# The feed-forward product of two batches by seven block products, with the sums of its weight blocks kept in DRAM and streamed

## The chip, the cores and the metric

The kernel runs on one core of one Trainium2 chip. The core has a matrix engine (PE, with its weight loads shown apart as PEld), a vector engine (DVE), a scalar engine (ACT), a third engine for elementwise work (POOL), and a queue (SP) from which nearly all DMAs are issued. The metric is the device time of one execution in microseconds (us); three executions of the kernel before gave 829.0, 829.38 and 829.86 us, median 829.38.

## The reference

There are 16 batches of 128 rows and 1024 columns. Each is normalised and goes through a cross attention with 32 query heads of width 32 and 8 key/value heads, with a residual; then the sum is normalised again and goes through one matrix product, again with a residual:

```python
x = x + xattn(layernorm(x), ctx, ctx, Wq, bq, Wk, bk, Wv, bv, Wo, bo)
x = x + scale * (x_ei @ kernel)        # x_ei: layernorm(x), its last 20% of columns times -4
```

`kernel` is a 1024 x 1024 matrix of zeros and ones (one in ten is a one). All the rest is float32. The second product is called the FFN below.

## The kernel before, in words

**Tiling.** Two batches make a group; there are eight groups. Of each group the kernel computes keys and values (`prep_k`, `prep_v`), queries (`prep_q`), the attention of four units (one batch and one half of the heads each: `scores`, `exponentials`, `divide`, `turn`, `weighted`), the output projection (`out_proj`) and the FFN (`ffn_transpose`, `ffn`).

**Seven products.** The query and output projections of a group are products of two-by-two blocks: 512 rows or columns of the weight against the halves of the two batches. `seven` (L385) does them by seven block products in place of eight. Each product accumulates in a PSUM tile, and `read` on DVE adds it to one of the four result blocks. The tile `u` takes products 1, 3, 5 and 7, and is read between them, so that product 3 can only start when the read after product 1 is over, and likewise 5 after 3 and 7 after 5. Product 2 has a tile of its own; products 4 and 6 share a third (`v`), which takes the buffer of product 2's tile (`ps_mm` has two buffers), so that product 4 waits for the read of product 2, and product 6 for that of product 4. Three of the seven products use plain weight blocks and four use sums of blocks. The sums are computed once (`combine`, L665), written to DRAM (`sums`) and streamed.

**The stream of weights.** `want` lists 512 KB pieces in the order in which they will be used; `fetch` (L202) issues the next piece's DMA into a ring of eight (`RING`) each time a piece has been used.

**The FFN before** takes each batch by itself. `ffn_transpose` (L614) turns the normalised rows by PE, ACT copies each half to a rounded copy `x2h` (type float32r), and DVE subtracts it to leave the remainder `x2l`. `ffn` (L630) multiplies both by the whole weight, which stays in SBUF in float32r (`wf_sb`): per batch two column halves, eight chunks, two parts, so 32 matmuls of 128 x 128 by 512. DVE then scales each half and adds the residual (L638).

**The order of the work** is written out ahead of time by a planner, `Stream` (L23). It keeps a clock, `now`. Dense work (products) comes from generators that give the time of each piece; `later(us, fn)` sets an event. Before each piece the events that are due are issued in the order of their due times. So every engine has one fixed queue in program order. A unit of attention issues its 32 score matmuls, adds 1.2 to the clock, sets four `exponentials` at 0.7, 3.1, 5.5 and 7.9 us after that, each `divide` 2.3 us behind its own, and each `turn` 9.25 us behind it in most groups (`length / 2 - 3`); it runs dense work until `length - 2` (22.5) us have passed, and closes with `weighted`, which adds 1.0. Groups 1 to 5 have this order, in the driver's `elif more` branch (L804 to L817): `out_proj` of the group before with `prep_ctx`, `prep_k`, `prep_v` with the four FFN transposes in it, the FFN of the two batches before, then `prep_x` and the queries of the next group. The third unit of a group begins just after the last value matmuls:

```python
mixed(prep_v(nxt), chain(ffn_transpose(p0), ffn_transpose(p1)), 1, 2),
once(get_x, nxt * GB + 1, 5.0),
```

`mixed(dense, light, skip, every)` puts a piece of the second generator behind each `every`th piece of the first, from number `skip` on. Group 6 has no FFN of its second batch, group 7 has units of 12 us, and the rest of the FFN stands at the end.

**Buffers.** Loaded rows are in `xn` (3 buffers), residuals in `x` (3), the FFN's parts in `x2h` and `x2l` (2 each), attention outputs in `yT` (7). The 0/1 weight is loaded as bytes (`load_ffn`) and converted on ACT (`convert_ffn`).

## Time and profile before

| what | value |
|---|---|
| median of three executions | 829.38 us |
| profiled execution: its time, its span | 829.15 us, 827.4 us |
| PE busy | 806.2 us, 97% of the span |
| DVE, ACT, POOL busy | 441.4 (53%), 350.7 (42%), 69.5 (8%) us |
| DMA | 165.14 MB, 200 GB/s over the span, q1 59% of the 16 engines |
| one group in the steady part (groups 2 to 5) | 100.2 us |
| last group (group 7), and what follows it | 58.8 us, 52.6 us |

The span is the time from the first instruction to the last; the 1.75 us between it and the execution's own time lie around it. In lists of groups of instructions, the first numbers are busy time in us and mean ns of one, and behind the second bar stands the idle time of the engine ahead of them and what ended it. In a timeline the columns are start and duration in us, engine, line, operation, output and inputs. Durations of DVE, ACT and PE overlap a little with the next instruction, so that the spacing of starts, not the duration, says what a row of instructions costs. A float32 matmul shows as two records, a float32r matmul as one.

### The profile page before, as it was taken

What the parts mean: (1) busy time and instruction counts of PE and PEld (TensorE: products, weight loads), DVE (VectorE), ACT (ScalarE), POOL (GpSimd) and SP (SyncE); (2) the same over time, 40 slices, a digit from 0 to 9 for tenths busy, and PEclk for the clock granted to TensorE, in tenths of its full rate; (3) what the DMA queues carried; (4) which work ended last, traced back from release to release, by engine and by line L of the source; (5) the groups of instructions that cost most, each with busy time, mean ns of one, the idle gap of its engine ahead of it and who ended that gap; (6) DMA issues with size and microseconds to landing.
All of it is one profiled execution on the core that took longest, in us unless ns stands there. A gap on an engine that the chain in (4) does not pass through costs nothing.

```text
span 827.4 us, 14055 instructions
## 1 busy us (share of the span) xinstructions
PE 806.2 (97%) x5344; PEld 606.9 (73%) x5344; DVE 441.4 (53%) x830; ACT 350.7 (42%) x1313; POOL 69.5 (8%) x110
## 2 busy tenths in 40 slices
PE   5999999999999999999999999999999999999997
PEld 4887884779757796588965889558895679756556
DVE  0469656555455554546564454654456555467442
ACT  1245854544335443445333543344434454366200
POOL 1000020002000020000200002000110002000300
PEclk9999999999999999999999999999999999999999
DMA  8899887416874088631886238860488407762511
GB/s 295 278 363 367 281 307 245 161 52 227 275 237 152 27 280 259 225 128 62 278 275 214 90 116 266 279 218 38 158 268 261 154 26 256 238 220 76 190 65 76
DMA packets 74082, 165.14 MB, mean 200 GB/s; under 512 B 5120, under 2 KB 33792, under 8 KB 74016
## 3 DMA queue, kind: packets, MB, share of 16 engines
q1 hardware_dynamic: 73728, 163.60, 59.0%
q8 instruction: 42, 0.69, 0.3%
q0 software_dynamic: 288, 0.66, 0.3%
q14 instruction: 24, 0.20, 0.1%
HBM read 147.46 MB, written 16.78 MB: 199 GB/s over the span
## 4 chain that ended last, share of the span: by engine, by line
PE 92%; DVE 2%; ACT 2%; issue 2%; DMA 1%; POOL 0%; SPq 0%; ACTq 0%; DVEq 0%; POOLq 0%
PE o_u L585 13%; PE f L282 13%; PE q_u L374 12%; PE tpp L524 7%; PE o_v L585 7%; PE q_v L374 6%; PE k L282 6%; PE v L282 6%; PE sc L491 4%; PE av L534 4%; PE q L282 3%; PE o_c L585 3%; PE q_c L374 3%; PE tp_f L624 2%; PE tp_x L299 1%
## 5 line engine op out<-in xcount | busy, mean ns | idle before, releaser
L507 ACT ACTIVATE p<-sc,negm 128x128 f32<-128x128 f32 x512 | 180.9, 369 | 163.2 <-DVE inv L518 97.1
L526 ACT COPY pt<-tpp 128x512 f32<-128x512 f32 x128 | 74.8, 592 | 91.6 <-PE tpp L524 91.3
L507 ACT ACTIVATION_READ_ACCUMULATOR p<-sc,negm 128x1 f32 x512 | 105.8, 207 | 0.0
L282 PE MATMUL f<-wf_sb,x2l 128*128 128x512 f32 x256 | 105.4, 412 | 0.0
L503 DVE TENSOR_REDUCE negm<-sc 128x4 f32<-128x512 f32 x128 | 86.7, 682 | 33.8 <-PE sc L491 33.7
L282 PE MATMUL f<-wf_sb,x2h 128*128 128x512 f32 x256 | 101.1, 395 | 0.0
L519 DVE TENSOR_TENSOR p<-p,inv 128x512 f32<-128x512 f32 x128 | 89.8, 701 | 4.4
L524 PE MATMUL tpp<-ident,p 128*128 128x128 f32 x512 | 77.4, 274 | 6.3 <-ACT pt L526 3.4
L374 PE MATMUL q_u<-t,piece 128*128 128x128 f32 x672 | 81.2, 275 | 0.0
L524 PEld LDWEIGHTS tpp<-ident,p 128*128 128x128 f32 x512 | 60.6, 141 | 25.3 <-issue 12.3
L374 PEld LDWEIGHTS q_u<-t,piece 128*128 128x128 f32 x672 | 78.0, 192 | 0.1
L282 PE MATMUL v<-wv_sb,cT 128*128 128x256 f32 x256 | 65.3, 390 | 4.9 <-DMA wv_sb<-in_L_xattn_Wv_dram 4.6
L166 POOL TENSOR_TENSOR x<-x,bo_b 128x256 f32<-128x256 f32 x64 | 48.2, 784 | 156.3 <-DMA x<-in_x_dram 154.9
L585 PE MATMUL o_v<-piece,s 128*128 128x512 f32 x128 | 60.2, 597 | 0.0
L585 PE MATMUL o_u<-piece,s 128*128 128x512 f32 x128 | 59.0, 593 | 0.0
L585 PE MATMUL o_u<-piece,yT 128*128 128x512 f32 x128 | 58.5, 599 | 0.0
L282 PE MATMUL k<-cT,wk_sb 128*128 128x256 f32 x256 | 58.3, 380 | 0.0
L282 PEld LDWEIGHTS f<-wf_sb,x2l 128*128 128x128 f32 x256 | 48.1, 188 | 11.0 <-issue 1.1
L282 PEld LDWEIGHTS f<-wf_sb,x2h 128*128 128x128 f32 x256 | 48.2, 188 | 10.3 <-issue 0.5
L542 ACT COPY yT<-av 128x512 f32<-128x512 f32 x32 | 18.7, 585 | 86.0 <-PE av L534 86.0
L282 PEld LDWEIGHTS v<-wv_sb,cT 128*128 128x128 f32 x256 | 47.1, 196 | 10.8 <-issue 5.0
L282 PEld LDWEIGHTS k<-cT,wk_sb 128*128 128x128 f32 x256 | 47.8, 190 | 9.0 <-issue 2.6
(80 smaller groups left out, 979.6 us busy)
## 6 DMA issues: line engine op xcount, KB each, us to landing
piece<-o SPq DMA_DIRECT2D x64, 512.0 KB, 4.6
piece<-q SPq DMA_DIRECT2D x56, 512.0 KB, 4.3
piece<-in_L_xattn_Wq_dram SPq DMA_DIRECT2D x50, 512.0 KB, 4.8
piece<-in_L_xattn_Wo_dram SPq DMA_DIRECT2D x48, 512.0 KB, 4.6
xn<-in_x_dram SPq DMA_DIRECT2D x16, 512.0 KB, 5.7
x<-in_x_dram SPq DMA_DIRECT2D x16, 512.0 KB, 5.6
out_dram<-x SPq DMA_DIRECT2D x16, 512.0 KB, 2.8
ctx<-in_ctx_dram SPq DMA_DIRECT2D x15, 512.0 KB, 7.2
```

What stands on the lines that cost most here:

```text
L166: lambda cut=cut: nc.gpsimd.tensor_add(x_t[:, cut], x_t[:, cut], bo_b[:, cut]) and None,
L282: nc.tensor.matmul(mm, lhsT=lhsT, rhs=rhs, start=k == 0, stop=k == n - 1)
L374: nc.tensor.matmul(mm if part is None else mm[:, part], lhsT=lhsT, rhs=rhs, start=start and n == k == 0, stop=k == len(some) - 1, skip_gro ...
L491: nc.tensor.matmul(tiles[i][:, g], lhsT=qT[rows, g], rhs=kT[rows, a, cols], start=True, stop=True,)
L503: nc.vector.tensor_reduce(negm, tile_, AX.X, ALU.max, negate=True)
L507: nc.scalar.activation(p[:, g], tile_[:, g], AF.Exp, bias=negm[:, g : g + 1], accum_out=total[:, g : g + 1],)
L519: nc.vector.tensor_mul(p, p, inv.unsqueeze(2).to_broadcast([P, NG, S]))
L524: nc.tensor.transpose(tp[:, g], p[:, g], ident)
L526: nc.scalar.copy(pt, tp)
L534: nc.tensor.matmul(mm[i * HD : (i + 1) * HD], lhsT=vs[b][:, h * HD : (h + 1) * HD], rhs=pts[i], start=True, stop=True,)
L542: nc.scalar.copy(yTs[b, a], mm)
L585: nc.tensor.matmul(mm, lhsT=lhsT[:, 2 * k + c], rhs=w[:, c], start=start and k == c == 0, stop=k == c == 1, skip_group_check=True,)
```

## The change

The FFN of a group is now done for both batches together by `seven`. Its left blocks are the halves of the two batches' normalised rows, its right blocks are the quarters of the weight. Three quarters (`b11`, `b21`, `b22`) stay in SBUF as float32r; the four sums are computed once on DVE from the byte weights, written to DRAM, and streamed through the ring like the other weights: eight pieces more for each group.

The transposes are now copied to `x2T` in float32 (ACT). Seven left operands (`a11`, `a12`, `a22` and four sums, made by DVE) are each split into a rounded copy by ACT and a remainder by DVE. `prepare` sets eight such steps as events; three more splits are set when products 1, 2 and 3 are done. `prepare` is issued in `prep_v`, behind the transposes, three pieces before its end.

Moved or resized around that: rows and residuals share one tag, `rows`, with seven buffers; both row loads of the next group are issued when a group begins and normalised 9 and 19 us later (before: 14 us, and 5 us after `prep_v`); two of the FFN transposes go into `prep_k`; the sums of Wq and Wo are handled and written as halves of 256 KB; `convert_ffn` starts after the last sums of Wo; the FFN of group 5 as a whole goes to group 7, those of groups 6 and 7 to the end; the first context tile and Wv are loaded by one DMA each instead of two; `bo_b` is loaded from SP, behind the first rows, instead of from POOL; `yT` has six buffers.

```diff
-    XB = 3
+    ROWS = 7
...
-    wf_sb = const.tile([P, NC, F], FR, name="wf_sb")
+    wf = {n: const.tile([P, NC // 2, HALF], FR, name=f"wf_{n}") for n in ("b11", "b21", "b22")}
...
-    load_ctx(0, 2)
-    for half in (slice(0, NC // 2), slice(NC // 2, NC)):
-        nc.sync.dma_start(
-            out=wv_sb[:, half], in_=Wv.rearrange("(c p) n -> p c n", p=P)[:, half]
-        )
+    load_ctx(0)
+    nc.sync.dma_start(out=wv_sb, in_=Wv.rearrange("(c p) n -> p c n", p=P))
...
-    nc.gpsimd.dma_start(out=bo_b, in_=bo.partition_broadcast(P))
     nc.gpsimd.dma_start(out=fscale, in_=ffn_scale.partition_broadcast(P))
+    nc.sync.dma_start(out=bo_b, in_=bo.partition_broadcast(P))
...
+        def convert(dst, c, cols):
+            src = raws[c // HC][:, c % HC, cols]
+            nc.scalar.activation(dst[:, c % HC], src, AF.Copy, scale=weights[c])
+
+        for c in range(HC):
+            stream.later(4.0 * c, lambda c=c: convert(wf["b11"], c, low))
+            stream.later(4.0 * c + 1.3, lambda c=c: convert(wf["b21"], c + HC, low))
+            stream.later(4.0 * c + 2.6, lambda c=c: convert(wf["b22"], c + HC, high))
+
+        def sums_of(k):
...
+            for (n, c), src in t.items():
+                cols = slice(c % 2 * HALF, (c % 2 + 1) * HALF)
+                nc.sync.dma_start(out=sums["f", n, k][:, cols], in_=src.bitcast(FP))
+
+        spread(sums_of(0), 1.8, lambda: spread(sums_of(1), 1.8))
...
-            cut = slice(4 * h, 4 * h + 4)
-            nc.scalar.copy(hi[:, cut], tp)
-            nc.vector.tensor_tensor(lo[:, cut], tp, hi[:, cut], ALU.subtract)
+            x2Ts[b, h] = work.tile(S4, FP, tag="x2T", name=f"x2T{b}_{h}", bufs=4)
+            nc.scalar.copy(x2Ts[b, h], tp)
             yield 0.45
...
+        def operand(n):
+            if n in half:
+                return half[n]
+            if n[0] == "a":
+                half[n] = x2Ts.pop((grp * GB + int(n[1]) - 1, int(n[2]) - 1))
+            else:
+                left, right, op = {
+                    "s1": ("a22", "a21", ADD),
+                    "s2": ("s1", "a11", SUB),
+                    "s3": ("a11", "a21", SUB),
+                    "s4": ("a12", "s2", SUB),
+                }[n]
+                left, right = operand(left), operand(right)
+                half[n] = work.tile(S4, FP, tag="comb", name=f"x{n}_{grp}", bufs=4)
+                nc.vector.tensor_tensor(half[n], left, right, op)
+            return half[n]
+
+        def split(n):
+            if n not in parts:
+                src = operand(n)
+                hi = work.tile(S4, FR, tag="x2h", name=f"x2h{grp}_{n}", bufs=4)
+                lo = work.tile(S4, FR, tag="x2l", name=f"x2l{grp}_{n}", bufs=4)
+                nc.scalar.copy(hi, src)
+                nc.vector.tensor_tensor(lo, src, hi, SUB)
+                parts[n] = lo, hi
+            return parts[n]
+
+        def prepare():
+            for n, (us, what, arg) in enumerate(
+                (
+                    (0.3, split, "a11"),
+                    (1.2, operand, "s1"),
+                    (2.0, operand, "s2"),
+                    (2.8, split, "a12"),
+                    (3.6, split, "s2"),
+                    (4.6, split, "s1"),
+                    (5.6, operand, "s3"),
+                    (6.6, operand, "s4"),
+                )
+            ):
+                stream.later(us, lambda what=what, arg=arg: what(arg) and None)
...
+            def product_of(prod, mm, start):
+                left, right = prod.split()
+                lhsTs = split(left)
+                for c in range(HC):
+                    if right in wf:
+                        w = wf[right][:, c]
+                    else:
+                        w = pieces[ids[prod, c // 2]][:, c % 2 * HALF : (c % 2 + 1) * HALF]
+                    for part in lhsTs:
+                        nc.tensor.matmul(
...
+                    if c % 2 == 1 and right not in wf:
+                        fetch()
+                    yield 0.47
+                done[0] += 1
+                if done[0] <= 3:
+                    late = ("s3", "s4", "a22")[done[0] - 1]
+                    stream.later(0.2, lambda: split(late) and None)
+
+            def read(mm, c):
+                j, h = int(c[1]) - 1, int(c[2]) - 1
+                x_t, cols = xs[b0 + j], slice(h * HALF, (h + 1) * HALF)
+                nc.vector.scalar_tensor_tensor(
+                    x_t[:, cols], mm, fscale, x_t[:, cols], MULT, ADD
+                )
+                reads[c] += 1
+                if c == "c21" or c == "c12" and reads[c] == 2:
+                    nc.sync.dma_start(out=out[b0 + j], in_=xs.pop(b0 + j))
+
+            yield from seven(f"f{grp}", product_of, read)
...
             elif more:
+                prepare, run = fs[grp - 1]
                 stream.add(
-                    once(get_x, nxt * GB, 14.0),
+                    once(get_x, nxt * GB, 9.0),
+                    once(get_x, nxt * GB + 1, 19.0),
                     mixed(os[grp - 1], prep_ctx(nxt), 6),
                     once(get_ctx, nxt + 1),
-                    prep_k(nxt),
-                    mixed(prep_v(nxt), chain(ffn_transpose(p0), ffn_transpose(p1)), 1, 2),
-                    once(get_x, nxt * GB + 1, 5.0),
+                    mixed(prep_k(nxt), ffn_transpose(p0), 4, 2),
+                    mixed(
+                        prep_v(nxt),
+                        chain(ffn_transpose(p1), once(prepare if nxt < NGRP - 1 else int)),
+                        1,
+                        2,
+                    ),
                 )
                 if nxt < NGRP - 1:
-                    stream.add(ffn(p0), mixed(ffn(p1), prep_x(nxt, 0), 12))
+                    stream.add(mixed(run, prep_x(nxt, 0), 22, 2))
                 else:
-                    stream.add(mixed(ffn(p0), prep_x(nxt, 0), 14))
+                    stream.add(prep_x(nxt, 0))
                 stream.add(once(residuals, grp), prep_x(nxt, 1), qs[nxt])
             else:
                 stream.add(
-                    os[grp - 1],
-                    mixed(ffn(p1 - 2), ffn_transpose(p0), 10, 2),
+                    between(os[grp - 1], 11, fs[grp - 2][0]),
+                    fs[grp - 2][1],
                     once(load_residual, b0, 2.0),
-                    mixed(ffn(p0), ffn_transpose(p1), 8, 2),
                     once(load_residual, b1, 2.0),
                 )
...
+            mixed(
+                between(os[b], 11, fs[a][0]),
+                chain(ffn_transpose(a * GB), ffn_transpose(a * GB + 1)),
+                2,
+            ),
+            mixed(
+                fs[a][1],
+                chain(ffn_transpose(b * GB), ffn_transpose(b * GB + 1), once(fs[b][0])),
+                14,
+                3,
+            ),
+            fs[b][1],
```

## The prediction

> **What bounds the kernel now.** I read the engines' shares first:
>
> ```profile
> span 827.4 us, 14055 instructions
> PE 806.2 (97%) x5344; PEld 606.9 (73%) x5344; DVE 441.4 (53%) x830; ACT 350.7 (42%) x1313; POOL 69.5 (8%) x110
> ```
>
> PE bounds it. Next, four stretches of one steady group: out-projection to values, the change of unit, the FFN, the queries.
>
> ```profile
> 345.80:369.10 23.30, 23.30 (x140) 18.06 (x136) 12.84 (x26) 11.54 (x42) 1.09 (x2) 1.00 0.47 158
> 369.10:371.60 2.50, 2.50 (x44) 1.51 (x44) 0.42 (x1) 0.58 (x1) 0.00 (x0) 1.00 0.00 0
> 371.60:389.70 18.10, 18.10 (x95) 14.88 (x94) 11.49 (x22) 9.34 (x39) 0.55 (x1) 1.00 0.08 30
> 389.70:421.40 31.70, 31.70 (x326) 29.55 (x324) 13.27 (x24) 10.76 (x41) 6.00 (x8) 1.00 0.83 267
> ```
>
> (Stretch, length, busy us of PE, PEld, DVE, ACT, POOL, granted clock, DMA share, GB/s.) PE has no gap; in the FFN DVE works 11.5 of 18.1 us, the DMA almost nothing. Then the groups by shape, for durations:
>
> ```profile
> L282 PE MATMUL f<-wf_sb,x2l 128*128 128x512 f32 x256 | 105.4, 412 | 0.0
> L282 PE MATMUL f<-wf_sb,x2h 128*128 128x512 f32 x256 | 101.1, 395 | 0.0
> ...
> L638 DVE SCALAR_TENSOR_TENSOR x<-f,fscale,x 128x512 f32<-128x512 f32 x32 | 23.9, 747 | 25.1 <-PE f L282 24.9
> ...
> L627 DVE TENSOR_TENSOR x2l<-tp_f,x2h 128x512 fp32r<-128x512 f32 x32 | 22.0, 692 | 55.8 <-ACT x2h L626 55.8
> ```
>
> The FFN is 512 matmuls. The last line is the one to remember: DVE stood still 55.8 us, 1.7 us a time, for the rounded copy that ACT had queued behind other work. Last, DVE's timeline at the start of an FFN, for spacings and order:
>
> ```profile
> 372.54 0.69 DVE L627 TENSOR_TENSOR x2l<-tp_f,x2h 128x512 fp32r<-128x512 f32 x1 [2.88 <-ACT x2h L626]
> 373.15 1.28 DVE L503 TENSOR_REDUCE negm<-sc 128x4 f32<-128x512 f32 x2
> 375.46 0.18 DVE L518 RECIPROCAL inv<-total 128x4 f32<-128x4 f32 x1 [1.03 <-ACT p L507]
> 375.68 0.69 DVE L519 TENSOR_TENSOR p<-p,inv 128x512 f32<-128x512 f32 x1
> 376.28 0.74 DVE L638 SCALAR_TENSOR_TENSOR x<-f,fscale,x 128x512 f32<-128x512 f32 x1
> 376.95 1.27 DVE L265 BATCH_NORM_STATS2 st_a<-xn 128x6 f32<-128x512 f32 x2
> ```
>
> A 128x512 subtraction costs 0.61 us, an FFN read 0.67 (376.28 to 376.95), a softmax maximum 0.60, a division 0.81. DVE stops where its next instruction isn't ready, whatever stands behind.
>
> **The change, part by part.** The sum is made against the profiled execution: 829.15 us, span 827.4; the median of the three runs is 0.2 us higher.
>
> *Matmuls.* A group's FFN goes from 64 to 7 x 4 x 2 = 56, in the whole kernel from 512 to 448. In the chain 46 of them take 10.74 us, 0.2335 each. Gain 64 x 0.2335 = 14.9 us, on the path.
>
> *DVE and ACT in a steady FFN.* DVE had 4 subtractions and 4 reads; now it has 4 sums, 7 subtractions, 7 reads: 11 x 0.61 + 7 x 0.67 = 11.4 us against 5.1. ACT goes from 4 copies to 4 + 7. A product takes 8 x 0.2335 = 1.87 us, one of the projections 3.43, and still waits for a read on DVE two products back. So order decides. By the planner's sums the second unit of a group stops three value pieces after the transposes, with one value piece left; `prepare` is set 1.85 us before the third unit's clock starts. On that clock things fall due: split a11 -1.55, s1 -0.65, s2 0.15, split a12 0.95, split s2 1.75, maximum and exponentials 0 at 1.9, split s1 2.75, s3 3.75, read 1 3.93, split s3 4.13, exponentials 1 4.3, division 0 4.35, s4 4.75, read 2 5.81, split s4 6.01, exponentials 2 and division 1 6.7, read 3 7.69, split a22 7.89, division 2 9.05, exponentials 3 9.1, read 4 9.57, division 3 11.4, read 5 after it. Nothing of it can be issued before the unit's closing and scores; so even a11 stands on ACT behind the attention copy (0.52 us, waiting for PE).
>
> I put these fixed queues beside each other with the spacings above, ACT copies 0.52, four exponentials 1.45, hand-overs 0.07 (ACT), 0.09 (DVE), 0.22 us (PE). Starts, in us from the closing matmuls of the second unit (369.1 in the trace before):
> - ACT: attention copy 1.2, a11 1.7, a12 2.3, s2 4.4, exponentials 0 6.5, s1 8.0, s3 9.9, exponentials 1 11.8, s4 13.2, exponentials 2 15.1, a22 16.6, exponentials 3 19.3.
> - DVE: rest of a11 2.3, s1 2.9, s2 3.6, rest of a12 4.3, value 4.9, rest of s2 5.2, maximum 0 5.8, rest of s1 8.6 (2.1 us idle: its copy is behind exponentials 0), s3 9.2, read 1 9.8, rest of s3 10.5, maximum 1, division 0, s4, read 2 13.1, rest of s4, maximum 2, division 1, read 3 15.8, rest of a22 17.2, division 2, maximum 3, read 4 19.2, division 3 20.8, read 5 21.6.
> - PE: P1 3.0, P2 5.0, P3 10.6 (idle 3.7, for read 1), P4 13.9 (idle 1.4, read 2), P5 16.6 (0.9, read 3), P6 19.9 (1.0, read 4), P7 22.4 (0.1).
>
> That is 7.3 us of idle PE where there was none, in the five FFNs of this order (groups 0 to 4, done in groups 1 to 5): 36.4 us. From below: if DVE never waits for ACT, the same queues give 2.7 us each (13.3); from above: with the full durations (0.08 us more each), 8.6 (43). I take 36.4, since the 55.8 us above show that it does wait. Late next are read 7 and the sums of the queries; two query products (7.1 us) cover these.
>
> *The three other FFNs.* That of group 5 lies where units last 12 us and DVE is busy 39.3 of 58.8 us; with 7 us more it must queue for some 30 us in 29: 3 us (0 to 5). That of group 6 has no softmax beside it but the second layernorms: 1 us (0 to 2). In the last, `prepare` comes 0.9 us ahead; by the same queues P2 waits 1.7, P3 0.7, P4 1.3 us: 3.7 (2 to 4).
>
> *Group 6* loses an FFN batch (7.5 us) under its last unit, whose softmax is then uncovered: 1.5 us (0 to 3).
>
> *Beginning.* Value matmuls start at 10.24, when the first half of Wv is there; halves landed 8.5 and 9.5 us after issue, the second at 11.6. Whole, Wv would come at 11.6; but `bo_b` (0.5 MB, landed over the same time) is gone from there, which at that slice's 295 GB/s is 1.8 us: 9.8, a gain of 0.4 (from 2.0, all of it ahead, to -1.4, none). `bo_b` on SP pushes the pieces of Wq by 1.8 us at most; the first was 8 us early.
>
> *Sums of the weight.* 16 DVE operations (9.8 us), 12 ACT conversions for 8, and some 40 more DMA issues on SP at 0.3 to 0.5 us; between 62 and 121 us DVE is busy 39.8 of 58.9. A tile of the second round must wait for a write. 1 us (0 to 3).
>
> *The stream.* 64 pieces, 33.6 MB more: a steady group goes from 189 to about 230 GB/s, 62 to 82 us showed up to 367. It fits in the FFN, where the DMA share is 0.08. Cost 0; uncovered it is a rival. *Moved loads:* both row loads stand on SP ahead of the out-projection's fetches; a wait there would hold them, but seven buffers serve six live tiles and the ring holds 8 x 1.72 = 13.8 us. The second normalisation (2.5 us of DVE) leaves the FFN for the out-projection, where DVE had a gap of 5.0 us. The transposes in `prep_k`, `yT` at six and the float32 copies cost nothing while PE has dense work of the same group beside them; uncovered, a transpose is 0.44 us.
>
> *Clock.* At the start PE idled 4.64 us, and the same 16 records then took longer than the next 16:
>
> ```profile
> 10.24 5.81 PE L282 MATMUL v<-wv_sb,cT 128*128 128x256 f32 x16 [4.64 <-DMA wv_sb<-in_L_xattn_Wv_dram]
> ...
> 17.17 3.72 PE L282 MATMUL v<-wv_sb,cT 128*128 128x256 f32 x16 [0.24 <-ACT cT L300]
> ```
>
> If the 3.7 us before P3 does that too, a stage costs up to 2.1 more, 10.5 in five; if not, nothing. I take nothing: it is shorter than the only gap shown. The Trainium skill ("TensorE: Matmul & The Clock Gate", the clock gate's "What's actually happening") says that the clock halves after an idle window of about 3.4 us, counted by a free-running window. By it such a gap may or may not hold a whole window, and the sum would be at most 5 x 1.7 = 8.5 us higher, which speaks against this change.
>
> *Sum.* -14.9 + 36.4 + 3 + 1 + 3.7 + 1.5 + 1 - 0.4 = +31.3; 829.15 + 31.3 = 860.4, by the median 860.6.
>
> **The rivals.**
> 1. *DVE has little to wait for on ACT* (chance 0.25). For: DVE is 53% busy. The five stages give 13.3: 829.4 - 14.9 + 13.3 + 9.8 = 837.6. Against: the order of split s1 behind exponentials 0.
> 2. *The other side: the splits hide* (0.12). If queues run ahead as in the out-projection, which has the same seven products without a gap, only the gain remains: 829.4 - 14.9 - 0.4 = 814. It decides below (14.9 - 9.8) / 5 = 1.0 us of idle PE for each steady FFN. Against: products half as long.
> 3. *The clock falls in each gap, or the weights come late* (0.06). Were all eight extra pieces moved in the query stretch (0.83 share, 8.5 MB in 31.7 us), 12.7 MB at 367 GB/s would take 34.6 us, 2.9 more for each of five to six groups: 15 to 17 us, or 10.5 from the clock; 870 to 878.
>
> **How the numbers follow.** The forecast has 0.53 and its own range 846 to 876 (terms at their ends); rival 1 has 0.25, rival 2 0.12, rival 3 0.06, and near no change, between rivals 1 and 2, 0.04. I say 860.5. The range 829 to 877 leaves out rival 2 and half of rival 3. A measurement of this kernel tells about 0.2% (1.7 us) from no change: faster 0.12, same 0.04, slower 0.84.
>
> **What would show it.** PE's idle in a steady FFN, 0 before: 7.3 us, the longest (3.7) ahead of the third product, ended by DVE's read. DVE's wait for ACT's rounded copies of s1, some 2 us each. PE busy near 791 us, 92% of the span. Value matmuls starting near 9.8. The prediction is wrong if the splits of s1 run before exponentials 0, if reads aren't what products wait for, or if PE waits for pieces.

## The result and the profile after

The changed kernel takes 875.27 us (median; 874.93 to 876.06) against 829.29 us for the kernel before on the same chip. The ratio is 1.0555, 95% interval [1.0537, 1.0573]: 5.6% slower. The forecast was 860.5 us, in a range of 829 to 877. The sign and the main mechanism were right; the size was 15 us short, and the time lies within 2 us of the range's upper end.

The first part of the profile of the changed kernel, engines by busy time:

```profile
span 874.2 us, 14292 instructions
PE 818.4 (94%) x5280; PEld 605.7 (69%) x5280; DVE 504.9 (58%) x926; ACT 379.7 (43%) x1373; POOL 73.9 (8%) x109
```

PE has 64 matmuls fewer and is still busy 12 us longer, since some of its matmuls ran at half clock (below). The same steady group in stretches: out-projection to values, from the change of unit through the FFN, the queries. The first line is of the kernel before, its whole stretch from out-projection to values (the prediction showed only the end of it); the others are of the changed kernel. The last line is the FFN stretch of another group, two groups later.

```profile
321.20:369.10 47.90, 47.37 (x225) 29.78 (x220) 27.96 (x54) 22.04 (x82) 1.64 (x3) 1.00 0.63 207
...
331.90:379.30 47.40, 46.87 (x224) 29.53 (x220) 28.24 (x56) 22.23 (x83) 2.19 (x4) 1.00 0.60 210
379.30:407.00 27.70, 23.50 (x134) 17.48 (x134) 18.56 (x33) 14.29 (x47) 0.00 (x0) 0.88 0.43 142
407.00:438.20 31.20, 31.20 (x322) 29.05 (x320) 13.39 (x22) 10.01 (x39) 6.94 (x8) 1.00 0.91 298
...
592.00:619.60 27.60, 21.14 (x133) 15.37 (x133) 18.52 (x33) 14.28 (x47) 0.00 (x0) 1.00 0.44 148
```

Before, the same work from the change of unit to the queries took 2.50 + 18.10 = 20.6 us and PE had no gap. Now it takes 27.7 us. DVE is busy 18.6 of these, so it is not full; the other two stretches are 0.5 us shorter each (47.9 and 31.7 before). The DMA share stays below one half here. So the loss is in the FFN. That it is neither DVE's sheer load nor the stream is what the experiments show below.

What PE waited for is in its timeline. Here is the FFN of the group whose stretch was the last line above, only the lines with a wait:

```profile
602.56 0.50 PE L720 MATMUL f_u<-piece,x2l_s 128*128 128x512 f32 x1 [3.17 <-DVE x L739]
...
606.03 0.49 PE L720 MATMUL f_v<-piece,x2l_s 128*128 128x512 f32 x1 [1.33 <-DVE x L739]
...
608.89 0.50 PE L720 MATMUL f_u<-piece,x2l_s 128*128 128x512 f32 x1 [0.77 <-DVE x L739]
...
612.26 0.51 PE L720 MATMUL f_v<-wf_b,x2l_s 128*128 128x512 f32 x1 [0.82 <-DVE x L739]
```

These are the third to sixth product, each waiting for a read (L739). And the reads were late because of this, in DVE's timeline of the first of the two groups; below it two lines of ACT's:

```profile
385.08 0.68 DVE L530 TENSOR_REDUCE negm<-sc 128x4 f32<-128x512 f32 x1
387.90 0.69 DVE L687 TENSOR_TENSOR x2l_s<-xs,x2h_s 128x512 fp32r<-128x512 f32 x1 [2.14 <-ACT x2h_s L686]
...
389.11 0.75 DVE L739 SCALAR_TENSOR_TENSOR x<-f_u,fscale,x 128x512 f32<-128x512 f32 x1
```

```profile
385.86 0.37 ACT L534 ACTIVATE p<-sc,negm 128x128 f32<-128x128 f32 x1 [1.58 <-DVE negm L530]
...
387.24 0.62 ACT L686 CAST x2h_s<-xs 128x512 fp32r<-128x512 f32 x1
```

The remainder of s1 stands next in DVE's queue, and its rounded copy is not made yet: ACT does the exponentials of the first softmax first, and before these it stood idle for 1.58 us, waiting for DVE's maximum. So each of the two engines waits for the other. The first product had ended by 384.5; its read, which needs nothing more, starts at 389.11, behind that wait. The third product starts at 389.91.

Where the 46.85 us between the two spans arose, from the start of each group's out-projection on PE:

| part | change | matmuls in it | stalls, after taking out the matmuls |
|---|---|---|---|
| up to the first query product | -1.66 | 0 | -1.66 |
| from the first query product to the first out-projection (sums of the weight) | +0.93 | 0 | +0.93 |
| five steady groups | +29.85 | -9.34 | +39.2 |
| group 6 | -7.04 | -7.47 | +0.4 |
| group 7 | +7.05 | -1.87 | +8.9 |
| what follows | +17.71 | +3.74 | +14.0 |

The matmuls are counted at 0.2335 us each. Two batches' transposes (1.8 us) went from group 7 into the part after it, which the last two rows do not take out; their sum, 22.9, is free of that.

### The profile page after: what moved, and what is told of

The parts are those of the page before. It is cut to its first block, busy times and chain, and to the rows that moved or that the text cites. A ratio compares the mean times of both kernels' runs of the same rounds, so it can differ in the third digit from the quotient of the medians.

```text
span 874.2 us, 14292 instructions
## 1 busy us (share of the span) xinstructions
PE 818.4 (94%) x5280; PEld 605.7 (69%) x5280; DVE 504.9 (58%) x926; ACT 379.7 (43%) x1373; POOL 73.9 (8%) x109
## 4 chain that ended last, share of the span: by engine, by line
PE 72%; DVE 12%; ACT 8%; DMA 5%; issue 1%; POOL 0%; SPq 0%; ACTq 0%; POOLq 0%; DVEq 0%
PE o_u L612 11%; PE q_u L401 11%; PE o_v L612 6%; PE tpp L551 6%; PE v L309 5%; PE k L309 5%; PE q_v L401 5%; ACT p L534 4%; PE sc L518 3%; PE av L561 3%; PE q_c L401 3%; PE q L309 3%; PE o_c L612 3%; DVE negm L530 2%; PE f_u L720 2%; DVE x2l_s L687 2%
## 5 line engine op out<-in xcount | busy, mean ns | idle before, releaser
L530 DVE TENSOR_REDUCE negm<-sc 128x4 f32<-128x512 f32 x128 | 87.2, 683 | 36.7 <-PE sc L518 36.4
L546 DVE TENSOR_TENSOR p<-p,inv 128x512 f32<-128x512 f32 x128 | 92.2, 720 | 4.4
L164 POOL TENSOR_TENSOR x<-x,bo_b 128x256 f32<-128x256 f32 x64 | 53.2, 861 | 282.7 <-DMA x<-in_x_dram 282.1
L612 PE MATMUL o_u<-piece,s 128*128 128x512 f32 x128 | 61.0, 608 | 3.8 <-DVE x L626 3.8
L518 PEld LDWEIGHTS sc<-kT,qT 32*128 32x128 f32 x1024 | 32.3, 190 | 26.0 <-issue 26.0
L720 PE MATMUL f_u<-piece,x2l_s 128*128 128x512 f32 x64 | 30.4, 475 | 17.4 <-DVE x L739 16.9
L612 PEld LDWEIGHTS o_u<-piece,yT 128*128 128x128 f32 x128 | 23.5, 190 | 28.4 <-issue 27.3
L612 PEld LDWEIGHTS o_u<-piece,s 128*128 128x128 f32 x128 | 23.3, 194 | 27.4 <-issue 22.3
```

The lines of the kernel that those rows point to most:

```text
L164: lambda cut=cut: nc.gpsimd.tensor_add(x_t[:, cut], x_t[:, cut], bo_b[:, cut]) and None,
L518: nc.tensor.matmul(tiles[i][:, g], lhsT=qT[rows, g], rhs=kT[rows, a, cols], start=True, stop=True,)
L530: nc.vector.tensor_reduce(negm, tile_, AX.X, ALU.max, negate=True)
L546: nc.vector.tensor_mul(p, p, inv.unsqueeze(2).to_broadcast([P, NG, S]))
L612: nc.tensor.matmul(mm, lhsT=lhsT[:, 2 * k + c], rhs=w[:, c], start=start and k == c == 0, stop=k == c == 1, skip_group_check=True,)
L720: nc.tensor.matmul(mm, lhsT=part[:, c], rhs=w, start=start and c == 0 and part is lhsTs[0], stop=c == HC - 1 and part is lhsTs[1], skip_gr ...
```

## The experiments

The first three each change one place of the changed kernel; the fourth takes the operand work away.

**The order of one split.** Only the due time of the split of s1 is moved, ahead of the first exponentials.

```diff
-                    (4.6, split, "s1"),
+                    (3.65, split, "s1"),
```

> The changed kernel (875.3 us) with one event of prepare moved: the split of s1 is due at 3.65 instead of 4.6 us, so that its rounded copy stands on ACT ahead of the exponentials of tile 0 and its remainder on DVE ahead of their maximum. Nothing else changes. Theory (order of the queues): the 2.1 us in which DVE stands still for that copy go from each of the five steady groups, and the read behind product 1 comes some 2 us earlier; by the queues laid side by side the idle time of PE falls from 7.3 to 6.0 us, because the reads behind products 2 and 3 then wait for other copies: five times -1.3, so about 869 us, and the wait ahead of product 3 is 1.6 us instead of 3.2. Rival (DVE is simply full there): the order of one copy makes no difference, 875. Rival (the halved clock is what costs): if the clock no longer falls because the gap is shorter than 3 us, a further 2 to 3 us each come back, 855 to 860.

864.38 us, ratio 1.0432 [1.0414, 1.0449]: 10.9 us less, with one event set 0.95 us earlier. Each steady group became 1.45 us shorter, 7.3 us in five (6.5 were expected), and group 7 with what follows 3.0 us, of which the expectation said nothing. PE's timeline, the waits of one FFN:

```profile
383.34 0.50 PE L720 MATMUL f_u<-piece,x2l_s 128*128 128x512 f32 x1 [0.93 <-DVE x L739]
387.59 0.50 PE L720 MATMUL f_v<-piece,x2l_s 128*128 128x512 f32 x1 [2.14 <-DVE x L739]
390.46 0.50 PE L720 MATMUL f_u<-piece,x2l_s 128*128 128x512 f32 x1 [0.73 <-DVE x L739]
393.83 0.50 PE L720 MATMUL f_v<-wf_b,x2l_s 128*128 128x512 f32 x1 [0.81 <-DVE x L739]
```

The four waits add up to 4.61 us instead of 6.09: the one ahead of the third product fell from 3.17 to 0.93, but the one ahead of the fourth grew from 1.33 to 2.14, and the 1.5 us that remain are the 1.45 that the group gained. The crossing of the two queues is a cause; behind it stands the next late operand. (The other 1.4 us of this kernel's gain lie ahead of the first out-projection, where nothing was edited. In the eight kernels that share this beginning the first query product came between 26.64 and 28.23 us. It goes with the moment at which PE's matmuls change from 0.43 to 0.22 us apart: 10.62 us in the kernel with the earliest, 13.75 in that with the latest, which is the changed kernel itself.)

**All operands earlier.** The second batch's two transposes come one and two value pieces earlier, `prepare` three: it now stands five pieces before the end of `prep_v`, and in the changed kernel two before it (not three, as written above).

```diff
                     mixed(
                         prep_v(nxt),
                         chain(ffn_transpose(p1), once(prepare if nxt < NGRP - 1 else int)),
+                        0,
                         1,
-                        2,
                     ),
```

> The changed kernel with the transposes of the second batch and prepare set two to three value pieces earlier (mixed ... 0, 1 instead of 1, 2), so that prepare stands some 5 us instead of 1.85 us ahead of the third unit, and the splits of a11, a12, s1 and s2 are issued before its scores. Nothing is left out. Theory (lead): with six of the eleven steps done beforehand the queues give 2.7 us of idle PE instead of 7.3 in each of the five steady groups: about 852 us, a steady group near 101.5 us instead of 106.3. Rival (amount of DVE work in the group, not its place): the work is the same, so the steady group stays within 1 us of 106: 870 to 875.

860.41 us, 1.0397 [1.0378, 1.0417]. A steady group takes 103.03 to 103.5 us, some 3 us less but 2 us more than was expected, and the whole is 8 us above its expectation. What is left is the late part of the queue: in the group looked at, PE waits 1.88 us ahead of the fourth product and 0.60 ahead of the sixth, and DVE waits for the rounded copies of s3 (1.48 us), s4 and a22 (0.61 each) with a read behind each. Group 6 lost 3 us (90.3 against 87.2): PE waits 1.42 us there for ACT's copy of transposed rows, and 3.4 us at half clock follow.

**The residual rows.** In the trace of the changed kernel DVE stands still for 8.93 us in the part after group 7, and SP shows why:

```profile
803.10 1.81 SPq L158 DMA_DIRECT2D x<-in_x_dram  x2
```

Both residual loads of the last group stand in the driver behind the FFN of group 5, which has become one piece; before, they were issued at 767.4 and 778.3, at the ends of single batches. This is DVE, and then PE:

```profile
815.02 0.69 DVE L626 TENSOR_TENSOR x<-o_u,x 128x512 f32<-128x512 f32 x1 [8.93 <-POOL x L164]
```

```profile
815.76 3.68 PE L612 MATMUL o_u<-piece,s 128*128 128x512 f32 x4 [3.81 <-DVE x L626]
```

The first read of the out-projection needs rows that POOL has not got yet. So one load was moved back:

```diff
                     between(os[grp - 1], 11, fs[grp - 2][0]),
-                    fs[grp - 2][1],
                     once(load_residual, b0, 2.0),
+                    fs[grp - 2][1],
                     once(load_residual, b1, 2.0),
```

> The changed kernel with the residual rows of the last group's first batch loaded ahead of the FFN of group 5 instead of behind it. In the trace after, the first read of the last output projection waits 8.9 us for POOL's addition on rows whose load was issued as that projection began; PE then stands 3.8 us and runs at half clock for 3.4 us. Theory (the load is late): the wait goes, -3.8 us, and with it the half clock, -1.7 us: 870 us, and the last stretch shortens from 70.3 to about 65. Rival (it is covered by something else that is as late): 874 to 875.

869.98 us, 1.0502 [1.0486, 1.0518]. The steady groups are the same within 0.1 us, and the part after group 7 went from 70.26 to 64.45 us, 5.8 less. It is the load's place in the queue.

**No operand work.** All seven products read the two parts of a11. The four sums and six of the seven splits are left out, so that this kernel computes something else; it has the same matmuls, reads and stream.

```diff
-                lhsTs = split(left)
+                lhsTs = split("a11")
...
-                done[0] += 1
-                if done[0] <= 3:
-                    late = ("s3", "s4", "a22")[done[0] - 1]
-                    stream.later(0.2, lambda: split(late) and None)
```

> The changed kernel with the FFN's operands left out but one: all seven products read the two parts of a11, so that the four sums and six of the seven splits are gone; the 56 matmuls for a group, the reads, the streamed pieces and the sums of the weight stay. The output is not the reference's. Theory (the steps that make the operands cost the time): the steady group falls below that of the kernel before by the eight matmuls saved, to about 98.5 us, and the whole to 815 to 827 us, below 829. Rival (the streamed weights, or reads between short products, cost it): the steady group stays above 100.2 and the whole above 835.

820.17 us, 0.9919 [0.9893, 0.9944]. The whole steady group of this kernel in the view of stretches, and below it the same group of the changed kernel:

```profile
314.52:413.25 98.73, 97.96 (x677) 74.32 (x673) 54.32 (x100) 43.16 (x163) 8.65 (x12) 1.00 0.68 236
```

```profile
331.88:438.22 106.34, 101.61 (x677) 76.09 (x673) 60.20 (x110) 46.53 (x169) 9.13 (x12) 0.97 0.65 218
```

With the operands goes nearly the whole stall: 98.3 to 98.7 us a group against 100.2 before, which is what 8 matmuls fewer are worth (1.87 us) within half a microsecond. Over the five groups the operands are 38.0 of the 39.2 us. Ten DVE instructions and six on ACT more are the difference between a gain of 1.5 us and a loss of 6. The stream, the short products and the seven reads cost next to nothing by themselves. Group 7 with what follows takes 119.1 us here, 136.2 in the changed kernel: the operands are 17.1 of the 22.9 us of stalls there. The rest is the residual load, which this kernel still has behind the FFN; PE waits 3.61 us for it.

**The work of the queue spread.** Here a11 and a12 are split in `prep_k`, three of the sums (s1, s2, s4) and their splits are set three value pieces earlier, the split tiles get five buffers, the operands of group 5's FFN move to group 6 and those of the last two FFNs start earlier too; the residual load is moved as above.

```diff
+            steps((0.3, split, "a11"), (1.0, split, "a12"))
...
+                (0.2, operand, "s1"),
+                (0.8, operand, "s2"),
+                (1.5, split, "s2"),
+                (2.0, operand, "s4"),
+                (2.6, split, "s1"),
+                (3.2, split, "s4"),
...
+                    mixed(prep_k(nxt), chain(ffn_transpose(p0), once(early)), 3, 2),
+                    mixed(prep_v(nxt), chain(ffn_transpose(p1), once(prepare)), 0, 1),
```

> The changed kernel with the operands of the FFN made earlier: a11 and a12 are split right after the transposes of the first batch, in prep_k; prepare stands two value pieces into prep_v; five splits (a11, a12, s2, s1, s4) are done before the FFN begins, which needs five buffers each for rounded copies and remainders instead of four (room from yT: four instead of six); only s3 and a22 are made beside the products, after products 1 and 2. The residual rows of the last group's first batch are loaded ahead of the FFN of group 5. Nothing of the computation is left out. Theory (the operands come too late, not too many): the steady group, 106.3 us in the changed kernel and 98.7 with one split, comes to 98.5 to 100.5, and the whole to 816 to 830 us, at or below the kernel before. Rival (DVE and ACT have too much to do in a group for the operands to be hidden anywhere): the group stays above 103, the whole above 845.

849.85 us, 1.0268 [1.0245, 1.0291]. A steady group takes 102.05 to 102.55 us, missing the expectation by 2 us, and the whole lies 20 us above it, where the rival had put it: the group fits neither, and some of the operand work is still not hidden. PE still waits 1.27 and 1.26 us ahead of the fourth and fifth product for a read. Group 6 became worse (94.84): PE waits 3.20 and 2.15 us there for ACT's copies of transposed rows, with 6.8 us at half clock.

Put back into group 7, all but the splits of a11 and a12, they give this:

> The kernel with early operands (849.9 us), with one thing put back: the operands of group 5's FFN beyond a11 and a12 are made in group 7 again, not in group 6. In the run with early operands group 6 took 94.8 us against 87.2 in the changed kernel, and in it PE waited 3.2 and 2.2 us for ACT's copies of transposed rows, which stood behind two rounded copies and a softmax, because in that group the row transposes follow prep_v at once. Theory (that is the loss): group 6 goes back to 87 to 88 us; group 7 takes up to 3 us more; the whole 843 to 846. Rival (the loss of group 6 is only moved to group 7): 849 to 850.

847.5 us, 1.0236 [1.0212, 1.0261]. Group 6 went back to 89.19 us, not to the 87.17 of the changed kernel, and group 7 with what follows grew from 122.9 to 127.3. So 4.4 of the 5.7 us were only moved, as the rival said; of the 2.6 us between the two spans, 1.4 lie ahead of the first query product, where nothing was edited.

**Another engine.** To the last kernel one thing is added: four of the seven remainders, and two of the sums, run on POOL.

```diff
-                nc.vector.tensor_tensor(half[n], left, right, op)
+                engine = nc.gpsimd if n in ("s3", "s4") else nc.vector
+                engine.tensor_tensor(half[n], left, right, op)
...
-                nc.vector.tensor_tensor(lo, src, hi, SUB)
+                engine = nc.vector if n in ("a11", "s1", "s2") else nc.gpsimd
+                engine.tensor_tensor(lo, src, hi, SUB)
```

> The same kernel as that with group 6 put back, and in it four of the seven remainders (a12, s3, s4, a22) and the sums s3 and s4 are made by POOL instead of DVE. POOL is busy 8% of the span; its additions of 128x256 take 0.72 to 0.86 us, so a step of 128x512 should take 1.45 to 1.7 us. Theory (what is left is DVE's work and its waits for ACT in front of the reads): the two waits of 1.3 us ahead of products 4 and 5 go, the steady group comes from 102.5 to 98.7 to 100.5 us, the whole to 822 to 832. Rival (POOL is too slow or gets in DVE's way at the shared memory port): the group stays at 102 or rises, the whole 843 or more.

831.13 us, 1.0045 [1.0029, 1.0061]: 16 us less. By shape, groups of POOL's and DVE's instructions:

```profile
L690 POOL TENSOR_TENSOR x2l_s<-xs,x2h_s 128x512 fp32r<-128x512 f32 x16 | 21.1, 1319 | 30.2 <-ACT x2h_s L688 30.2
...
L690 DVE TENSOR_TENSOR x2l_s<-xs,x2h_s 128x512 fp32r<-128x512 f32 x16 | 14.5, 933 | 7.2 <-ACT x2h_s L688 7.1
...
L690 DVE TENSOR_TENSOR x2l_a<-x2T,x2h_a 128x512 fp32r<-128x512 f32 x8 | 5.5, 691 | 20.4 <-ACT x2h_a L688 20.4
```

On POOL a remainder takes 1.32 us, on DVE 0.69, so by work this is a loss. But much of the waiting for ACT is now POOL's, and no read of DVE's stands behind it. (DVE also has less to do: it is busy 58.2 us in a steady group for 60.5, and the group is 2.3 us shorter. This run alone doesn't tell waiting from work; that the same work costs less in another order is shown by the first two experiments.) A steady group takes 99.8 to 100.2 us, with one wait of 0.21 us for a read left in its FFN, and no half clock remains. That is 1.5 us above the kernel without operand work, and on average only 0.1 us under the kernel before. Group 7 with what follows takes 121.0 us, against 111.4 before.

**The beginning.** The prediction had `bo_b` taking bandwidth from Wv. Two kernels, both the kernel before with one edit: `bo_b` issued from SP as in the change; and the first context and Wv by one DMA each.

> The kernel before with bo_b alone moved: loaded from SP behind the first rows instead of from POOL ahead of them. Theory (bo_b took bandwidth from Wv): the value matmuls start earlier than 10.24 us, and the first query matmul (29.89 before, 28.2 after the whole change) comes 1 to 1.7 us earlier, the whole 1 to 1.7 us shorter. Rival (one DMA instead of two for Wv is what helps): the first query matmul stays at 29.9.

829.19 us, 1.0009 [0.9993, 1.0025]. The halves of Wv land at 10.52 and 11.89 us (10.11 and 11.61 before). `bo_b` is not the cause.

> The kernel before with Wv and the first context tile loaded by one DMA each, bo_b still from POOL. Theory (bo_b took the bandwidth): the value matmuls start when the second half came before, at about 11.6 instead of 10.24 us, and the first query matmul comes up to 1.4 us later than 29.89; the whole is 0 to 1.4 us longer. Rival (the single DMA helps): they start before 9.5 us and the whole is shorter by 1 to 1.7 us.

826.36 us, 0.9983 [0.9972, 0.9994]. Wv lands at 7.65 us, with `bo_b` still in its old place. So it is one of the two DMAs, and the next pair takes one each:

```diff
-    for half in (slice(0, NC // 2), slice(NC // 2, NC)):
-        nc.sync.dma_start(
-            out=wv_sb[:, half], in_=Wv.rearrange("(c p) n -> p c n", p=P)[:, half]
-        )
+    nc.sync.dma_start(out=wv_sb, in_=Wv.rearrange("(c p) n -> p c n", p=P))
```

> The kernel before with the value weight by one DMA and the first context still by two. Theory: the halves of the value weight themselves move slowly (10.11 and 11.61 us in the kernel before, against 7.65 whole); then the weight lands at 7.5 to 8.3 us, the value matmuls start near 7.8 to 8.5 instead of 10.24, the first q matmul comes near 28.2 to 28.8 instead of 29.89, and the whole is 826.2 to 827.5 us. Rival: the two small DMAs of the first context are what slows the beginning; then the weight lands no earlier than 9.5 us and the whole stays within 0.5 us of the kernel before.

```diff
-    load_ctx(0, 2)
+    load_ctx(0)
```

> The kernel before with the first context by one DMA and the value weight still by two. Theory (halves of the weight are slow): the second half lands at 11 to 12 us, the first q matmul comes at 29.5 to 30.2 us and the whole is within 0.5 us of the kernel before. Rival (the split context is the cause): both halves have landed by 9 us, the first q matmul comes before 28.7 us and the whole is 826 to 827 us.

Wv whole alone: 831.4 us, 1.0032 [1.0019, 1.0046], slower than before. The context whole alone: 824.9 us, 0.9946 [0.9929, 0.9962], the fastest kernel here that computes what the reference does. My theory fell and the rival stands. PE's first lines, of the kernel with Wv whole alone and then of that with the context whole alone:

```profile
3.49 2.23 PE L296 MATMUL tp_c<-ident,ctx 128*128 128x128 f32 x8 [3.49 <-DMA ctx<-in_ctx_dram]
12.15 6.49 PE L279 MATMUL v<-wv_sb,cT 128*128 128x256 f32 x16 [6.42 <-DMA wv_sb<-in_L_xattn_Wv_dram]
```

```profile
4.77 1.94 PE L299 MATMUL tp_c<-ident,ctx 128*128 128x128 f32 x8 [4.77 <-DMA ctx<-in_ctx_dram]
6.53 5.84 PE L282 MATMUL v<-wv_sb,cT 128*128 128x256 f32 x16
```

The context by two DMAs lets the transposes start 1.1 to 1.3 us sooner, and everything behind it comes later: Wv whole lands at 12.01 us instead of 7.65. With the context whole, the first half of Wv lands at 6.06, before the transposes are over, and the second at 8.60. From 4 to 8 us the core moved 364 and 285 GB/s with both whole, 195 and 279 with the context split. Why the split context costs the DMAs behind it so much was not found. Each of these landing times is from one trace.

Last, the POOL version with Wv in two halves again, its context whole as in the change:

> The seven-product kernel with half of the operand work on POOL (831.13 us), and now the beginning that was best in the last pair: first context by one DMA, value weight by two halves. If that beginning carries over, the value matmuls start near 6.5 us instead of 7.8, the first q matmul comes 1.2 to 2 us sooner and the whole is 829 to 830 us, the same as the kernel before within 0.2% and still above the 824.9 us of the kernel before with that beginning alone. If it does not carry over (the pieces of Wq behind it are what the queries wait for), it stays at 830.5 to 831.5 us.

829.64 us, 1.0016 [1.0004, 1.0029]. The first query product comes 1.5 us sooner (26.33 after 27.85), and so does the end. (26.33 here and 26.20 with the context whole alone are sooner than in any of the eight kernels with Wv whole.) So the FFN by seven products, with its operands on two engines and its residual load moved, comes back to where the kernel before stands. The kernel that beats both is the one before with its first context by one DMA.

## Why the prediction was right, and where it was not

*Matmuls (-14.9 us).* Right. Without operand work the steady groups were 1.4 to 1.9 us shorter than before, where 1.87 was counted.

*DVE and ACT in a steady FFN (+36.4).* Right in mechanism and size: 39.2 us by the table, 7.5 to 8.0 a group for 7.3 (the waits that the prediction lists add up to 7.1). In the group shown above the waits were 3.17, 1.33, 0.77 and 0.82 us ahead of the third to sixth product, for 3.7, 1.4, 0.9 and 1.0. They count less than they cost: set matmul by matmul beside the kernel without operand work, the four products begin another 3.4, 1.5, 1.0 and 1.1 us late, 7.6 in all with 0.3 ahead of the second. DVE's wait for the copy of s1 was 2.14 us for 2.1, and its cause, the exponentials ahead of it on ACT, is shown by the one-line edit of its due time. One reason given for taking 36.4 and not 13.3 was a misreading, though: that DVE waited 55.8 us in the kernel before for copies that ACT had queued behind other work. ACT itself stood idle there, waiting for PE's transposes:

```profile
L626 ACT CAST x2h<-tp_f 128x512 fp32r<-128x512 f32 x32 | 18.7, 589 | 55.5 <-PE tp_f L624 55.5
```

The line showed no crossing of the two queues; the queues laid side by side did, and the choice was right because of them.

*Clock (0).* Right for the steady groups, though the clock did fall. In four of the five the third product's wait was followed by 6.83 us at half clock, as here, with starts 0.43 us apart where they had been 0.23:

```profile
389.91 0.80 PE L720 MATMUL f_u<-piece,x2l_s 128*128 128x512 f32 x1 [3.17 <-DVE x L739]
390.50 0.63 PE L720 MATMUL f_u<-piece,x2h_s 128*128 128x512 f32 x1
390.93 0.63 PE L720 MATMUL f_u<-piece,x2l_s 128*128 128x512 f32 x1
...
399.62 0.51 PE L720 MATMUL f_v<-wf_b,x2l_s 128*128 128x512 f32 x1 [0.66 <-DVE x L739]
```

The fifth, whose waits were shown first, had full clock (1.00 in its stretch, 0.88 in the other) and was as long: 106.33 us against 106.34 and 106.31. The slow matmuls filled the waits ahead of the fourth and fifth product, and the sixth started 20.3 us after the change of unit in both. My reason, that the gap was shorter than the one gap shown, was wrong twice. Gaps far shorter made the clock fall, and the gap shown was no example: PE was slow there before it, too (the eight transposes ahead of it took 1.94 us, the next eight 1.04), and with the context whole alone the same 16 matmuls took 5.84 us with no gap ahead of them. The forecast of PE's busy time (791 us; it was 818.4) failed mostly by this: the POOL version, without half clock, shows 798.8.

What decides, as far as these traces tell, is where the gap lies. The traces record when the granted clock changes, and in each kernel all these moments lie a whole number of times 3.413 us apart. Here are two such windows of the changed kernel, one at whose end the clock fell, and the one that held most of the fifth group's gap:

```profile
385.80:389.21 3.41, 0.94 (x5) 0.42 (x3) 1.31 (x3) 2.01 (x9) 0.00 (x0) 1.00 0.00 0
...
600.84:604.25 3.41, 1.69 (x7) 1.41 (x8) 3.28 (x7) 0.93 (x3) 0.00 (x0) 1.00 0.00 0
```

By its busy time PE was idle for 72% of the first and 50% of the second. Between 30 us and the last 3 us of all the kernels the clock fell at the end of 25 windows: PE was idle for 55 to 100% of 24 of them and 49% of one, and for at most 54% of every other window at full clock. The Trainium skill ("TensorE: Matmul & The Clock Gate", "What's actually happening") says that the clock falls after an idle window of about 3.4 us that runs freely. The fixed spacing agrees with a window that runs freely. But most of the windows here were not idle throughout, and gaps of 2.14 and 1.88 us did it too (last section); where these differ from the page, the measurement decides.

*The three other FFNs (+3, +1, +3.7).* Wrong in size: the step failed here. The operands cost 17.1 us in group 7 and after it, and 7.7 were predicted. Set matmul by matmul beside the kernel without operand work, whose PE does the same work in the same order, the last FFN lost 4.0 us for 3.7 (waits of 1.44, 0.45 and 1.23 us) and that of group 6 2.1 for 1 (waits of 0.92 and 0.33). Group 7, where the FFN of group 5 lies, lost 10.9 for 3:

```profile
776.54 0.69 DVE L687 TENSOR_TENSOR x2l_s<-xs,x2h_s 128x512 fp32r<-128x512 f32 x1 [2.08 <-ACT x2h_s L686]
...
778.20 0.97 PE L551 MATMUL tpp<-ident,p 128*128 128x128 f32 x4 [4.27 <-DVE p L546]
...
782.36 0.80 PE L720 MATMUL f_c<-wf_b,x2l_a 128*128 128x512 f32 x1 [1.48 <-DVE x L626]
```

I had put DVE's 7 us more against its free time there, an average. But its queue stands in order, and the same crossing (2.08 us for a copy of ACT's, at 776.54) now delays a softmax division, and with that PE's transposes of the attention: two paths are late, not one. I had worked out the steady queue item by item and this one by its sum. Of the 10.9 us, 4.4 come with the wait at 778.20, 1.5 with that at 782.36, and some 3.5 while the clock was at half, from 778.3 to 788.6 us. The half clock is no cost of its own here either: in the kernel with the residual load moved it lasted 3.4 us at this place instead of 10.2, and group 7 was as long (66.1 us against 65.9), with waits of 1.57 and 0.91 us ahead of later transposes instead.

*Moved loads (0).* Wrong: +5.8 us. I counted buffers and fetches of the loads at a group's start, and did not look where the last group's residual loads stood once the FFN ahead of them was a whole group's. In the trace of before the first was issued 7.4 us ahead of the group's out-projection (767.44 against 774.81), in that of after 0.8 us (803.10 against 803.94).

*Group 6's uncovered softmax (+1.5):* +0.4. *Sums of the weight (+1):* +0.93 from the first query product to the first out-projection, one wait of 0.91 us: a softmax division stood in DVE's queue behind a sum that waited 3.14 us for a write, as the prediction had feared. It isn't there every time: without operand work, and in the kernels with five buffers, the same part is 0.2 us shorter than before. *Stream (0):* right, shown by the kernel without operand work.

*Beginning (-0.4).* Right in sign, by luck, wrong in cause and size: -1.66 us, and up to -3.25 in the other kernels that begin like this. The whole context did it, of which the prediction said nothing, and Wv by one DMA took part of it back.

*Rivals.* The first (DVE has little to wait for) and the second (the splits hide) are refuted by the waits. The third came to a time near the one measured (870 to 878) by another way: its clock fell without costing, and its weights were not late. So the right time alone would not have told the forecast from this rival; the waits do.

The prediction's terms in the runs' numbers: -14.9 + 39.2 + 0.4 + 17.1 + 5.8 + 0.93 - 1.66 = +46.9 us, the difference of the spans.

## What to carry to other kernels

Where two engines pass work to each other in fixed order, lay the two queues beside each other item by item in every stage, not only in the steady one: an engine that is half idle still stops everything behind one operand that another engine makes late. Here it helped to move the waiting instruction, earlier or to an engine with nothing urgent behind it, even one that needs twice the time, without saving any work. When a piece of work grows, look at every load that is issued behind it; and when transfers at the beginning are split to start sooner, measure what the split does to those behind them.

## What was not expected of the hardware

- The clock falls after gaps of PE that are far shorter than the 4.64 us of the prediction, and whether it falls depends on where the gap lies in windows of 3.41 us. The steady FFN, five times in each kernel, with its longest gap: 3.17 us, half clock in four of five; 2.14 us (one split moved), four of five; 1.88 us (operands earlier), two of five; 1.27 us (queue spread), none.
- Two DMAs of 256 KB for the first context, ahead of Wv, made Wv land 4.4 us later than one DMA for the same bytes (12.01 for 7.65, one trace each).
- While POOL made four of the remainders, DVE's of s1 and s2 took 0.93 us instead of 0.69, and its normalisations of the second layernorm 0.96 us instead of 0.86. The gain of 16 us came in spite of that.
